# Attention in half chunks with heads by twos, and fewer routing operations a turn, in a fused attention and expert kernel

## The chip, the cores and the metric

The kernel runs on one core of one Trainium2 chip, in one launch. The metric is the time of the launch on the device in microseconds (us), the median of several runs. The engines are PE (matrix products), DVE (elementwise work and reductions), ACT (activation functions and copies), POOL (GpSimd), and SP, which here only issues DMAs. All data are fp32.

## The reference

One layer is computed: attention, then a feed-forward part with experts, each with a residual sum and a layer norm. The input `x` is 16 sequences of 512 tokens of 128 features; there are 16 heads of 8 features.

```python
q, k, v = silu(x @ Wq), silu(x @ Wk), x @ Wv            # split into heads
q, k = lrpe(q), lrpe(k)                                  # [t*cos(theta*pos), t*sin(theta*pos)], 8 -> 16
energy = einsum('bhnd,bhmd->bhnm', q, k) * tril(ones)    # no softmax
out = einsum('bhnm,bhmd->bhnd', energy, v) @ Wo
out = layernorm(out * sigmoid(x @ G1 @ G2)) * gamma + beta
x = layernorm(x + out)
...
# feed-forward: 8 experts, two for each token, at most 1280 tokens for each expert, and a shared part
probs = softmax(rmsnorm(x) @ router_w.T); top 2; weights normalised
routed = sum over both experts of weight * (silu(x @ rg) * (x @ ru)) @ rd
shared = silu(x @ sg) * (x @ su) @ sd
x = layernorm(x + shared + routed)
```

Since there is no softmax, attention is linear: the keys and values of all earlier tokens can be summed up in one small matrix for each head (a "state"), and only the tokens of one's own chunk need the masked product.

## The kernel before

**Stages.** Attention runs first, by turns of one chunk of 128 tokens (64 turns, four chunks for each sequence), and the routing of the tokens is woven into it. A loop behind attention ends the routing and the scatter of the tokens to their experts. Then come the eight experts, and last the sums and the final layer norm. The shared feed-forward part is cut into half steps (`shared_steps`, each 0.86 us of PE: one product with `sg` or `su`, or half of one with `sd`), which lie in a list, `feed`. They are taken from it by all stages: two in a turn, one in each step of the loop behind attention, and all that are left in the end stage.

**Order.** PE, DVE, ACT and POOL run their instructions in the order in which the program issues them (`manual_schedule`). The loop over `t` issues, in this order: `project(t + 2)` (products with the weights, `pq`, and their activations and copies on ACT, then `hat`, the keys and queries times cosine and sine, on DVE); a shared half step; three operations of routing (`sprinkle`); `turn_over(t + 1)` (transposes, `pt`, and on ACT the copies `kT`, `q2`, `qT`); a shared half step; a part of the output side of an earlier sequence (`after`, driven by `advance`); `energies(t)`; `values(t - 1)`; `remember(t + 1)`; two scatters on POOL; further parts of `after`; four operations of routing.

**PSUM.** There are two pools of four banks: `ps_e` for the energies (`pe`), and `ps_w` for everything else, which is taken in turn by `pq`, `pg`, `pt`, `pu`, `pout`, `pst` and the products of `after` and `route`. A new tile waits until the tile four before it has been read.

**Energies and values.** A chunk is cut into two halves of 64 tokens. The keys of every second head (the "late" heads) lie with their halves exchanged, so that the two halves of the 128 key rows hold different heads. `energies` makes three blocks of 64 queries for each group of heads: the first queries with the first keys, the last with the first, the last with the last. `q2` holds six blocks of the queries, with every second head put to zero by the two columns of `par`. The products are masked by `causal` into `et` on DVE. `values` multiplies them with padded copies of the values (`vpad`, and `vlow` for the first half), 24 products of 64 columns, and adds the state of all earlier chunks, 4 products of 128 columns.

**Memory.** `remember` multiplies keys and values of a chunk (8 products over 128 rows), masks the result with `bmask` on DVE, and adds it on POOL to the state so far. The last chunk of a sequence needs none.

**Routing.** `route` runs for three groups of sequences (0 to 5, 6 to 11, 12 to 15). It is a generator with some 33 operations, nearly all on DVE.

**Experts and end.** `clear_rows` puts rows of an expert's tile that hold no token to zero (DVE), and `turn_rows` transposes them (PE). `finish_lot` makes the last layer norm for four chunks or, for the last sequence, for one: statistics on DVE, `rstd_of` (a power on POOL) or, once the table of roots is on ACT, `rstd_by_root`, then `nb` on DVE and the output on ACT. `an_end` advances the first three unfinished lots; a lot that yields False lets the next one go.

Of the kernel before, what the change touches and what calls it, by code (L numbers as in the profile page):

```python
# [19 lines left out]
P = 128  # L20
# [18 lines left out]
PI_BELOW = 3.141592  # L39

# [6 lines left out]
def tile_kernel(  # L47
# [146 lines left out]
    with ExitStack() as ph:  # L194
# [21 lines left out]
        with tc.manual_schedule(engines=ORDERED):  # L216
# [51 lines left out]

            NVP = 4
            vpads = []  # L270
            for i in range(NVP):
                vp = cst.tile([P, 4, 4, 40], F32, name=f"vpad{i}")

                vl = cst.tile([P, 8, 40], F32, name=f"vlow{i}")
                vpads.append((vp, vl))
                if i < 2:
                    nc.gpsimd.memset(vp, 0.0)
                    nc.gpsimd.memset(vl, 0.0)
# [11 lines left out]
            for vp, vl in vpads[2:]:  # L290
                nought(vp.rearrange("p a b d -> p (a b d)"), 640)
                nought(vl.rearrange("p a d -> p (a d)"), 320)
# [24 lines left out]

        def sines(c):

            for s, (from_, scale, bias) in enumerate([(scratch[:, NC + c], -1.0, half_pi), (scratch[:, c], 1.0, 0.0)]):  # L320
                for to, n0, n1 in ((cst_tok[:, c, 0], 0, D), (cst_tok[:, c, 1, 1::2], D, D + HALF)):
                    nc.scalar.activation(
                        to[:, :, s, :], from_[:, n0:n1].rearrange("p (h d) -> p h d", d=8), AF.Sin,
                        scale=scale, bias=bias,
                    )

        def same(c):

            nc.vector.tensor_copy(
                cst_tok[:, c, 1, 0::2].rearrange("p h s d -> p h (s d)"),  # L330
                cst_tok[:, c, 0, 0::2].rearrange("p h s d -> p h (s d)"),
            )

        with tc.manual_schedule(engines=ORDERED):
# [7 lines left out]
            causal = cst.tile([P, 3, HALF], F32, name="causal")  # L342
            nc.gpsimd.tensor_tensor(causal[:, 0, 0:1], scratch[:, 0, 0:1], zcol, ALU.mult)
            nc.gpsimd.memset(causal, 1.0)
            bmask = cst.tile([P, 64], F32, name="bmask")
            nc.gpsimd.memset(bmask, 1.0)
            nc.gpsimd.affine_select(
                bmask, bmask, pattern=[[-16, 8], [0, 8]], compare_op=ALU.is_ge, fill=0.0, base=0, channel_multiplier=1
            )
            nc.gpsimd.affine_select(  # L350
                bmask, bmask, pattern=[[16, 8], [0, 8]], compare_op=ALU.is_ge, fill=0.0, base=15, channel_multiplier=-1
            )
            for block, at in ((0, 0), (0, HALF), (1, HALF), (2, 0)):
                rows = causal[at : at + HALF, block, :]
                nc.gpsimd.affine_select(
                    rows, rows, pattern=[[1, HALF]], compare_op=ALU.is_ge, fill=0.0, base=0, channel_multiplier=-1
                )
# [50 lines left out]
        hats, qkt, ets, states, gates, oTs = {}, {}, {}, {}, {}, {}  # L408


        def project(t):
# [11 lines left out]
            nc.scalar.activation(qk[:, D:].rearrange("p (h d) -> p h d", d=16), pq[:, 0:8, 16:32], AF.Silu)  # L423
            if c == 0:
# [4 lines left out]
            vp, vl = vpads[t % NVP]  # L429
            nc.scalar.copy(  # L430
                vp.rearrange("p a (c b) d -> p (a c) b d", b=2)[:, :, :, 0:8],
                pq[:, 8:16, 16:32].rearrange("p h (b d) -> p h b d", b=2),
            )
            for i in range(2):
                mine = slice(HALF * i, HALF * i + HALF)
                nc.scalar.copy(vl[mine, :, 8 * i : 8 * i + 8], pq[mine, 8:16, 16 + 8 * i : 24 + 8 * i])
# [10 lines left out]
        def turn_over(t):  # L447
# [9 lines left out]
            q2 = wk2.tile([P, 2, 6, HALF], F32, tag="q2", name=f"q2_{t}")  # L457
            halves = pt[:, 0].rearrange("p a (h n) -> p a h n", h=2)
            nc.scalar.activation(q2[:, :, 0:5:4, :], halves, AF.Copy, scale=par[:, 0:1])
            nc.scalar.activation(q2[:, :, 3:6:2, :], halves, AF.Copy, scale=par[:, 1:2])  # L460
            nc.scalar.copy(q2[:, :, 1:3, :], q2[:, :, 4:6, :])
# [4 lines left out]
        def remember(t):  # L466

            b, c = divmod(t, NC)
            hat = hats.pop(t)
            if c + 1 == NC:  # L470
                return
            vp = vpads[t % NVP][0]
            pst = ps_w.tile([P, 2, 64], F32, tag="w", name=f"pst_{t}")
            for s in range(2):
                for i in range(4):
                    nc.tensor.matmul(
                        pst[32 * i : 32 * i + 32, s, :], hat[:, 1, ds(s * P + 32 * i, 32)],
                        vp[:, 2 * s : 2 * s + 2, :, 0:8], start=True, stop=True,
                    )
            states[t] = new = wk3.tile([P, 2, 64], F32, tag="state", name=f"state_{t}")  # L480
            mask = bmask.unsqueeze(1).to_broadcast([P, 2, 64])
            if c == 0:
                nc.vector.tensor_tensor(new, pst, mask, ALU.mult)
            else:
                add = wk2.tile([P, 2, 64], F32, tag="add", name=f"add_{t}")
                nc.vector.tensor_tensor(add, pst, mask, ALU.mult)
                nc.gpsimd.tensor_tensor(new, states[t - 1], add, ALU.add)

        def energies(t):

            kT, q2, _ = qkt[t]
            pes = [ps_e.tile([P, 2, 3, HALF], F32, tag="e", name=f"pe_{t}_{g}") for g in range(4)]
            for s in range(2):
                for g in range(4):
                    rows = slice(32 * g, 32 * g + 32)
                    for i in range(2):
                        mine = slice(HALF * i, HALF * i + HALF)
# [612 lines left out]
```

## Time and profile before

| | |
|---|---|
| median of 3 runs | 874.49 us (873.55 to 876.25) |
| the profiled execution | 865.53 us |
| its span | 863.8 us |
| mean granted clock of PE | 0.988 of full |
| PE, DVE, ACT, POOL busy | 825.7, 554.2, 433.0, 337.2 us |
| attention turns | from about 15 us to 375 us |
| loop behind attention | to about 518 us |
| experts | to about 741 us |
| end stage | to 863.8 us |

In the rows of the profile, `L498` is line 498 of the kernel; `out<-in` are the program's names; `32*64 32x192` is a tile of 32 rows and 64 columns of the PE array that a moving matrix of 32 rows and 192 columns passes through. An fp32 product is carried out as two instructions, so the counts of matmuls are twice those of the code. In a group, the numbers after the bar are the busy time in us and the mean ns of one, then the idle time of the engine before them and who ended it. In a timeline, the numbers are start and duration in us. In a list of waits, they are us in total, how often, and the longest.

### The profile page before, as it was taken

The numbers are of one execution on the slowest core, as the hardware profiler recorded it, in microseconds if no ns is written. First come the engines' busy times: TensorE is split into PE (matmuls) and PEld (weight loads), VectorE is DVE, ScalarE is ACT, GpSimd is POOL, SyncE is SP. The second block draws the span as 40 slices with busy tenths as digits, with TensorE's granted clock in tenths as the row PEclk, the third lists the DMA queues.
The fourth block names the chain that finished last, engine by engine and source line by source line (L and its number), as shares of the span: only waits on it lengthen the run. The fifth ranks groups of instructions, "written<-read, shape, count | busy, mean of one in ns | idle before, by whom it ended". The sixth has DMA issues, their size and how long they took to land. (4 is left out here: it accounts for less than half of the span.)

```text
span 863.8 us, 24377 instructions
## 1 busy us (share of the span) xinstructions
PE 825.7 (96%) x9776; PEld 568.8 (66%) x9776; DVE 554.2 (64%) x1629; ACT 433.0 (50%) x1279; POOL 337.2 (39%) x451
## 2 busy tenths in 40 slices
PE   6899999989999998899999998999999999999896
PEld 4666668756766865756666665777667776755664
DVE  7887888889988788975533335444434442387754
ACT  6876776675677677544222222333333333243345
POOL 2132122221666665587666641343333433211110
PEclk9999999999999999999999999999999999999999
DMA  6011111110111110048000032231122200365211
GB/s 199 21 34 33 34 33 33 34 33 15 51 56 56 59 46 21 21 163 295 22 10 6 0 99 79 94 95 53 63 90 93 62 28 25 92 178 169 78 37 49
DMA packets 66387, 57.45 MB, mean 67 GB/s; under 512 B 6180, under 2 KB 55132, under 8 KB 66274
## 3 DMA queue, kind: packets, MB, share of 16 engines
q1 hardware_dynamic: 59474, 44.95, 17.1%
q0 software_dynamic: 6656, 10.69, 3.8%
q8 instruction: 77, 1.26, 0.6%
q10 hardware_dynamic: 144, 0.26, 0.1%
q14 instruction: 36, 0.29, 0.1%
HBM read 32.62 MB, written 26.48 MB: 68 GB/s over the span
## 5 line engine op out<-in xcount | busy, mean ns | idle before, releaser
L725 POOL DMA_INDIRECT xg_dram<-x,idx x128 | 132.3, 1034 | 42.7 <-issue 40.9
L936 POOL DMA_INDIRECT y_dram<-y,to x80 | 77.6, 970 | 155.3 <-ACT y L934 155.3
L138 ACT ACTIVATE sl<-pg 128x512 f32<-128x512 f32 x128 | 75.6, 594 | 121.4 <-PE pg L136 114.7
L150 DVE TENSOR_TENSOR h<-sl,pu 128x512 f32<-128x512 f32 x128 | 87.6, 684 | 74.8 <-PE pu L149 57.7
L136 PE MATMUL pg<-x1T,sg_sb 128*128 128x512 f32 x256 | 132.2, 598 | 0.0
L149 PE MATMUL pu<-x1T,su_sb 128*128 128x512 f32 x256 | 130.9, 593 | 0.0
L159 PE MATMUL pd<-sd_sb,h 128*128 128x128 f32 x1024 | 125.1, 279 | 5.9 <-DVE x1T L164 5.7
L505 DVE TENSOR_TENSOR et<-pe,causal 128x384 f32<-128x384 f32 x256 | 124.4, 547 | 9.1 <-PE pe L498 8.7
L159 PEld LDWEIGHTS pd<-sd_sb,h 128*128 128x128 f32 x1024 | 121.3, 195 | 12.1 <-DVE x1T L164 6.3
L1024 DVE TENSOR_TENSOR eh<-esl,peu 128x512 f32<-128x512 f32 (+1 forms) x96 | 57.5, 599 | 109.8 <-PE peu L1021 107.2
L112 POOL TENSOR_TENSOR rstd<-ve,neghalf 128x4 f32<-128x4 f32 x46 | 49.5, 1076 | 195.1 <-DVE ve L110 188.8
L930 PEld LDWEIGHTS ped<-rd,eh 128*128 128x128 f32 x640 | 84.0, 192 | 24.1 <-issue 22.0
L1019 PE MATMUL peg<-xgT,rg 128*128 128x512 f32 (+1 forms) x192 | 84.6, 522 | 0.0
L1021 PE MATMUL peu<-xgT,ru 128*128 128x512 f32 (+1 forms) x192 | 84.4, 521 | 0.0
L930 PE MATMUL ped<-rd,eh 128*128 128x128 f32 x640 | 84.3, 275 | 0.0
L1023 ACT ACTIVATE esl<-peg 128x512 f32<-128x512 f32 (+1 forms) x96 | 50.5, 526 | 57.5 <-PE peg L1019 54.8
L149 PEld LDWEIGHTS pu<-x1T,su_sb 128*128 128x128 f32 x256 | 45.9, 191 | 44.9 <-issue 39.9
L934 ACT ACTIVATE y<-ped,wt 128x128 f32<-128x128 f32 x80 | 29.4, 367 | 85.7 <-PE ped L930 85.7
L136 PEld LDWEIGHTS pg<-x1T,sg_sb 128*128 128x128 f32 x256 | 44.7, 192 | 37.4 <-issue 34.1
L415 PE MATMUL pq<-W,xT 128*128 128x384 f32 x128 | 59.9, 551 | 7.5 <-DVE h L150 3.2
L498 PE MATMUL pe<-q,kT 32*64 32x192 f32 x2048 | 62.6, 340 | 0.8 <-DVE et L505 0.8
L1021 PEld LDWEIGHTS peu<-xgT,ru 128*128 128x128 f32 x192 | 36.5, 190 | 32.2 <-issue 28.9
(181 smaller groups left out, 1250.8 us busy)
## 6 DMA issues: line engine op xcount, KB each, us to landing
y_dram<-vpad SPq DMA_DIRECT2D x16, 512.0 KB, 7.3
y<-y_dram SPq DMA_DIRECT2D x32, 256.0 KB, 3.3
xT<-xt SPq DMA_DIRECT2D x15, 384.0 KB, 2.9
xg<-xg_dram SPq DMA_DIRECT2D x8, 660.0 KB, 4.5
x<-x SPq DMA_DIRECT2D x16, 256.0 KB, 3.5
o<-res SPq DMA_DIRECT2D x15, 256.0 KB, 2.8
xg_dram<-x,idx POOLq DMA_INDIRECT x128, 2.3
rg<-rg SPq DMA_DIRECT2D x8, 256.0 KB, 4.7
```

Of the source, the lines that this page charges most:

```text
L136: nc.tensor.matmul(pg, sg_sb[:, ts(i, P)], seq, start=True, stop=True)
L138: nc.scalar.activation(sl, pg, AF.Silu)
L149: nc.tensor.matmul(pu, su_sb[:, ts(i, P)], seq, start=True, stop=True)
L150: nc.vector.tensor_tensor(h[i // half][:, i % half, :], h.pop(("s", i)), pu, ALU.mult)
L159: nc.tensor.matmul(pd, h[k][:, i - k * half, ts(c, P)], sd_sb[:, i, :], start=(i == 0), stop=(i == IS // P - 1))
L498: nc.tensor.matmul(pes[g][mine, s], kT[rows, s, mine], q2[rows, s, 3 * i : 3 * i + 3], start=(s == 0), stop=(s == 1),)
L505: nc.vector.tensor_tensor(et.rearrange("p s k n -> p s (k n)"), pes[g].rearrange("p s k n -> p s (k n)"), causal.rearrange("p k n -> p (k ...
L725: i = nc.gpsimd.indirect_dma_start(out=xg_dram[:, :], out_offset=bass.IndirectOffsetOnAxis(ap=idx[:, k, t : t + 1], axis=0), in_=x1[:, t, ...
L930: nc.tensor.matmul(pd, h[:, i, ts(c, P)], got[e][2][:, i, :], start=(i == 0), stop=(i == IR // P - 1))
L936: i = nc.gpsimd.indirect_dma_start(out=y_dram[:, :], out_offset=bass.IndirectOffsetOnAxis(ap=to[:, at : at + 1], axis=0), in_=y, in_offset ...
L1019: nc.tensor.matmul(pg[:, :n], rg_sb[:, ts(i, P)], xgTs[e][:, ds(o0, n)], start=True, stop=True)
L1021: nc.tensor.matmul(pu[:, :n], ru_sb[:, ts(i, P)], xgTs[e][:, ds(o0, n)], start=True, stop=True)
```

## The change

- The two halves of a chunk are treated as chunks of their own. `energies` makes for each half only the block of its own queries and keys, 128 columns for each product (two kinds of head by 64) in place of 192. `q2` has four blocks in place of six, and one copy on ACT falls away. `causal` is one triangle.
- `remember` keeps a state for the middle of each chunk (`mids`) besides the one for its end (`lasts`): two products of 64 rows in place of one of 128, two masked products on DVE and two sums on POOL, and also for the last chunk of a sequence (its middle alone).
- `values` adds a state for each half (8 products of 64 columns) and needs 16 other products in place of 24. There is one padded tile of values in place of two; ACT fills it by four copies of 64 rows.
- The late heads come in twos (two early, two late) in place of one by one; the host arranges `Wk`, `Wv`, `Wo` and `theta` to fit, and ACT writes the key activations by two instructions.
- A turn does two and three operations of routing in place of three and four.
- Four shared half steps are issued between clearing and transposing the rows of the first expert.
- A lot that waits for its root on POOL yields False until three half steps have begun, in place of one turn that counts as work.

In the new program's order, the loop behind attention and the four steps hold 168 shared half steps (156 before), the expert stage 3 (3 before) and the end stage 111 (123 before).

```diff
@@ project
-            vp, vl = vpads[t % NVP]
-            nc.scalar.copy(
-                vp.rearrange("p a (c b) d -> p (a c) b d", b=2)[:, :, :, 0:8],
-                pq[:, 8:16, 16:32].rearrange("p h (b d) -> p h b d", b=2),
-            )
-            for i in range(2):
-                mine = slice(HALF * i, HALF * i + HALF)
-                nc.scalar.copy(vl[mine, :, 8 * i : 8 * i + 8], pq[mine, 8:16, 16 + 8 * i : 24 + 8 * i])
+            vp, v = vpads[t % NVP], pq[:, 8:16, 16:32].rearrange("p k (u d) -> p k u d", u=2)
+            for half in range(2):
+                mine = slice(HALF * half, HALF * half + HALF)
+                for u in range(2):
+                    nc.scalar.copy(vp[mine, :, half ^ u, 8 * u : 8 * u + 8], v[mine, :, u, :])
@@ turn_over
-            nc.scalar.activation(q2[:, :, 0:5:4, :], halves, AF.Copy, scale=par[:, 0:1])
-            nc.scalar.activation(q2[:, :, 3:6:2, :], halves, AF.Copy, scale=par[:, 1:2])
-            nc.scalar.copy(q2[:, :, 1:3, :], q2[:, :, 4:6, :])
+            for i in range(2):
+                nc.scalar.activation(q2[:, :, :, i, :], halves, AF.Copy, scale=par[:, i : i + 1])
@@ remember
-            if c + 1 == NC:
-                return
-            vp = vpads[t % NVP][0]
-            pst = ps_w.tile([P, 2, 64], F32, tag="w", name=f"pst_{t}")
+            pst = [ps_w.tile([P, 2, 64], F32, tag="w", name=f"pst_{t}_{half}") for half in range(2)]
             for s in range(2):
                 for i in range(4):
-                    nc.tensor.matmul(
-                        pst[32 * i : 32 * i + 32, s, :], hat[:, 1, ds(s * P + 32 * i, 32)],
-                        vp[:, 2 * s : 2 * s + 2, :, 0:8], start=True, stop=True,
-                    )
+                    for half in range(2 if c + 1 < NC else 1):
+                        rows = slice(HALF * (half ^ i % 2), HALF * (half ^ i % 2) + HALF)
+                        nc.tensor.matmul(
+                            pst[half][32 * i : 32 * i + 32, s, :], hat[rows, 1, ds(s * P + 32 * i, 32)],
+                            vp[rows, 4 * s : 4 * s + 4, half, 0:16], start=True, stop=True,
+                        )
...
+            for half, kept in enumerate((mids, lasts) if c + 1 < NC else (mids,)):
+                kept[t] = new = wk3.tile([P, 2, 64], F32, tag=f"state{half}", name=f"state_{t}_{half}")
+                add = new if state is None else wk2.tile([P, 2, 64], F32, tag=f"add{half}", name=f"add_{t}_{half}")
+                nc.vector.tensor_tensor(add, pst[half], mask, ALU.mult)
+                if state is not None:
+                    nc.gpsimd.tensor_tensor(new, state, add, ALU.add)
+                state = new
@@ energies
-                    for i in range(2):
-                        mine = slice(HALF * i, HALF * i + HALF)
+                    for k in range(2):
+                        mine = slice(HALF * k, HALF * k + HALF)
+                        half = k ^ g % 2
                         nc.tensor.matmul(
-                            pes[g][mine, s], kT[rows, s, mine], q2[rows, s, 3 * i : 3 * i + 3],
+                            pes[g // 2, half][mine, s], kT[rows, s, mine], q2[rows, s, half],
                             start=(s == 0), stop=(s == 1),
                         )
@@ values
+            for half in range(2):
+                cols = slice(HALF * half, HALF * half + HALF)
+                state = mids.pop(t) if half else lasts.pop(t - 1, None)
+                for g in (0, 2, 1, 3) if state is not None else ():
+                    s, a = divmod(g, 2)
                     nc.tensor.matmul(
-                        pout[32 * a : 32 * a + 32, :], state[:, s, ts(a % 2, 32)], qT[:, s, :],
-                        start=True, stop=False,
+                        pout[32 * g : 32 * g + 32, cols], state[:, s, ts(a, 32)], qT[:, s, cols],
+                        start=(half == 0), stop=False,
                     )
...
@@ the turns
-                sprinkle(t, 3)
+                sprinkle(t, 2)
...
-                sprinkle(t, 4)
+                sprinkle(t, 3)
@@ finish_lot
             yield True
-            if not roots:
-                yield True
+            at = begun
+            while not roots and feed and begun < at + 3:
+                yield False
@@ the first expert
             for o0, n in parts:
                 clear_rows(0, o0, n)
+            for _ in range(4):
+                feed.pop(0)[2]()
             for o0, n in parts:
                 turn_rows(0, o0, n)
```

## The prediction

> **What bounds the kernel now.** I read the page's first part, then the waits of PE, then the busy table of two stretches of the attention stage, then PE's timeline of two turns, then the groups by shape.
>
> ```profile
> span 863.8 us, 24377 instructions
> ...
> PE 825.7 (96%) x9776; PEld 568.8 (66%) x9776; DVE 554.2 (64%) x1629; ACT 433.0 (50%) x1279; POOL 337.2 (39%) x451
> ```
>
> PE is busy for 96% of the span. Whether its few idle stretches have a cause that the change touches is told by its waits:
>
> ```profile
> PE pd L159 <- DVE x1T L164: 5.7, 3, 2.9
> PE po L555 <- ACT vlow L436: 4.2, 2, 2.1
> PE pq L415 <- DVE h L150: 3.2, 2, 1.9
> PE ept L906 <- DVE h L150: 2.5, 1, 2.5
> ```
>
> Three waits in the end stage (5.7 us), two at the exponentials of routing (4.2), two in the routing turns (3.2), one ahead of the first expert (2.5). Nothing waits turn by turn. The busy table of two stretches in the middle of attention says the same (columns: PE, weight loads, DVE, ACT, POOL, clock, DMA):
>
> ```profile
> 100.00:140.00 40.00, 40.00 (x850) 27.14 (x852) 34.46 (x109) 29.80 (x105) 8.25 (x10) 1.00 0.09 26
> 140.00:180.00 40.00, 40.00 (x864) 29.97 (x867) 32.48 (x100) 28.43 (x101) 10.14 (x12) 1.00 0.10 29
> ```
>
> PE is full; DVE has 14 to 19% left. So a saving on PE in a turn is a saving in time as long as DVE's turn shrinks with it. What the steps of a turn cost on PE is read from start to start, because matmuls overlap:
>
> ```profile
> 122.80 0.91 PE L498 MATMUL pe<-q,kT 32*64 32x192 f32 x32
> 123.63 0.43 PE L531 MATMUL pout<-et,vlow 128*32 128x64 f32 x16
> 123.88 0.63 PE L540 MATMUL pout<-et,vpad 128*32 128x64 f32 x32
> 124.33 0.41 PE L476 MATMUL pst<-vpad,hat 128*32 128x64 f32 x16
> 124.67 0.66 PE L602 MATMUL px<-ident,x 128*128 128x128 f32 x4
> ...
> 128.28 0.91 PE L498 MATMUL pe<-q,kT 32*64 32x192 f32 x32
> 129.11 0.43 PE L522 MATMUL pout<-qT,state 128*32 128x128 f32 x8
> 129.36 0.41 PE L531 MATMUL pout<-et,vlow 128*32 128x64 f32 x16
> 129.58 0.63 PE L540 MATMUL pout<-et,vpad 128*32 128x64 f32 x32
> 130.03 0.40 PE L607 MATMUL plg<-x1T,rw_sb 128*32 128x128 f32 x8
> ```
>
> Energies take 0.83 us. Values take 129.11 to 130.03, 0.92 us, with a state and 0.70 without. L540's 32 instructions of 64 columns on four tiles (128 rows by 32 columns) take 0.45, so a round over the four tiles takes 0.056 us and the instructions start 14 ns apart. The memory step (L476) is four such rounds, 0.22, but 0.34 pass before the next step: changing the tile shape costs about 0.12.
>
> **Part by part, on PE.** *Energies*, 64 turns: the same 32 instructions on the same eight tiles (32 rows by 64), with 128 columns instead of 192. By the 0.056 of 64 columns, 192 take about 0.16 a round; four rounds are 0.64 of the 0.83, and 0.19 does not depend on columns. New: 4 x 0.107 + 0.19 = 0.62. Saving 0.21 x 64 = 13.4 us. *Values*: with a state, before 4 state matmuls of 128 columns (worth eight of 64) and 24 of 64 columns, 16 rounds' worth; after, 8 state and 16 others of 64, 12 rounds. Saving 4 x 0.056 = 0.22 in 48 turns, 10.8. In the 16 first chunks 12 rounds become 10: 0.11 x 16 = 1.8. *Memory*: the three chunks that had 8 matmuls now have 16, each over 64 rows, so that eight tiles (64 by 32) can run at once. No row shows this shape. Bounds: eight at once, four rounds as now, 0; four at once, eight rounds, +0.22. I take 0, because the eight tiles of L498, also split by rows, overlap. But values (128 rows) and memory (64 rows) now differ in shape, and between them comes one more change of 0.12 (bounds 0 and 0.17, half more than read): 0.12 x 48 = 5.8. The last chunk of a sequence, which had none, gets 4 rounds and a change: 0.34 x 16 = 5.4. Sum on PE: -13.4 - 10.8 - 1.8 + 5.8 + 5.4 = **-14.8 us**; between -22 (shape changes free) and -4 (four tiles at once, 0.22 x 48 = +10.6).
>
> The Trainium skill's page "TensorE: Matmul & The Clock Gate", section "Wait — 56ns, not 53.3ns?", says that matmuls never start less than about 25 ns apart, however small. By it the 32 instructions of the new memory step would take 0.80 us, and the 48 steps 28 us more than I count, an estimate that would turn the change into a loss; the 14 ns of L540 contradict it for neighbouring tiles, and I follow the row.
>
> **On the other engines.** They matter only if they become later than PE.
>
> ```profile
> L505 DVE TENSOR_TENSOR et<-pe,causal 128x384 f32<-128x384 f32 x165 | 80.2, 547 | 7.1 <-PE pe L498 6.9
> L461 ACT COPY q<-q 128x256 f32<-128x256 f32 x42 | 17.0, 405 | 1.3
> L487 POOL TENSOR_TENSOR state<-state,add 128x128 f32<-128x128 f32 x20 | 9.1, 457 | 45.7 <-DVE add L486 21.3 <-DVE sq L593 16.4 <-DVE nb L582 5.5
> L594 DVE TENSOR_TENSOR sq<-sq,mv 128x4 f32<-128x4 f32 x10 | 4.2, 422 | 0.3
> L593 DVE TENSOR_TENSOR sq<-rstd 128x4 f32<-128x4 f32 x10 | 1.5, 153 | 0.0
> ```
>
> DVE: the four masked products of a turn go from 384 to 256 elements. With 278 ns for the 128 elements of L486 an element costs (547 - 278)/256 = 1.05 ns, so each saves 0.13 and a turn 0.54; one more product with `bmask` in every turn costs 0.28. Net -0.26 a turn, as much as PE's -14.8/64 = -0.23, so DVE keeps its distance. ACT: the copy of 405 ns goes; the keys come in two halves (0.27 to 2 x 0.215) and the values in four pieces (0.71 to 4 x 0.215), together +0.31; net -0.1 a turn. POOL: 96 state sums instead of 32, 64 x 0.457 = 29 us more, within the 13 to 15 of 40 us that it has idle in the scatter turns (busy 25.4 and 27.0 of 40 from 220 to 300); the sum for a chunk is made a turn before its values need it.
>
> One price of these sums falls on DVE. L594 takes 422 ns where L593, of the same four elements, takes 153: it runs just as POOL starts its sum, and waits 0.27. Such a hit can come in every turn: at most 64 x 0.457 = 29 us on DVE, 0.46 a turn, against the 0.9 that it has left of 5.4 (14 to 19%). So it is hidden in plain turns; in the turns with routing it is not. I take +1 us (0 to +6, the loss where a quarter of the 29 falls in full turns). The skill's "SBUF — State Buffer", section "Who interferes with whom", has this rule: a DVE instruction with two inputs in SBUF and a GpSimd one that reads SBUF block each other wholly. By it every sum that meets such an instruction would cost DVE its 0.457, rather than the 0.27 of the row.
>
> **Routing by five** operations a turn: 2 + 3 for 3 + 4. The same operations (about 0.36 each) are spread over seven turns rather than five, so DVE overruns a turn by 0.7 less. Of PE's 3.2 us at `pq`, plus 0.5 and 0.4 in the same turns, I expect half: **-2** (-4 to 0). The exponentials stay in the same turn, and with them the 4.2. The scatters of the second group start two turns later, so four more of them are left for the loop behind attention, which then takes eight more shared half steps: PE works through them as before, they are only taken from the end stage.
>
> **Rows cleared sooner.** Four shared half steps (0.86 each) go between clearing and transposing expert 0's rows. PE's wait of 2.5 at `ept` should be filled. But the first of them is a down step whose bank was last read by a DVE addition that is queued behind the clearing, so part of the wait stays in front of it. **-1** (-2.5 to 0).
>
> **The end stage.** 111 shared half steps remain instead of 123, with the same 64 rows of statistics and sums behind them. DVE waits 9.2 us there for POOL's roots (nine times, up to 1.2); now other work of the next lots is queued meanwhile, which should undo some of PE's 5.7 us at `pd`: -3 (-5.7 to 0). Against it: in the new order the last four-chunk lot and all four single lots finish behind the last down step, and ACT's four outputs (1.65 us) stand before the first single root: +1.9. Sum **-1** (-4 to +3).
>
> The opening loses two fills of 320 elements on ACT (0.46 each); the chain there goes through DVE's angles, so 0.
>
> **The sum.** -14.8 + 1 - 2 - 1 - 1 = -17.8 us. Against the profiled execution's own 865.5 (span 863.8 and 1.7 around it) that is 847.7. The median of the runs, 874.5, lies 9.0 above that execution; I keep the difference and predict **856.7 us**.
>
> **Rivals.** *Small tiles don't overlap.* The memory step runs four at a time: +10.6, so -7.2 and 867. For it: no row has 64 by 32. Against it: the eight tiles of L498. Chance 0.18. *The stalls go too.* The lighter DVE removes all of PE's waits in routing, at `ept` and at `pd`, and shape changes are free: -22 - 4 - 2.5 - 4 = -32.5, 842. For it: every one of these waits names DVE. Against it: two of them are tied to queue order. Chance 0.12. *PSUM becomes the bound: slower.* A turn now takes seven buffers from the ring of four at `ps_w`, and the next chunk's `pt` reuses the one of the first state product; so PE waits at `pt` until DVE has done four `et` and that product. Now the product is needed only at the next shared step. In the turn of 133.69 it ends at 137.72, and `pt` starts at 137.64; after the change the product ends 0.54 sooner and `pt` starts about 0.3 sooner, a margin of 0.16 us. If POOL's sums hold DVE back by more than that in every turn, PE pays the rest: from 0.16 + 17.8/64 = 0.44 on, the gain is gone; at 0.9 a turn the loss is 0.74 x 64 = 47, less 17.8, so +30 and 904. Against it: DVE has 0.9 left in a plain turn. Chance 0.06.
>
> **How the numbers follow.** Forecast 0.60 (846 to 863 by the bounds of its smaller terms); small tiles 0.18; stalls gone 0.12; ring 0.06; the rest, 0.04, is all terms cancelling within 0.3%, about what a measurement of this kernel can tell from no change. The range of 845 to 869 takes in the forecast and the small tiles, and leaves out the ring and most of the largest gain. Faster by over 0.3%: 0.60 + 0.18 + 0.12 = 0.90; same 0.04; slower 0.06.
>
> **What would show it.** In the changed profile: energies from start to start about 0.62, values about 0.70, memory about 0.34 with a gap of 0.1 before it; `et` near 413 ns; no row of PE waiting at `pt` for a state product; turns near 5.1 where they were 5.3 to 5.5. A memory step of over 0.5, or `pt` waits of tens of microseconds, would prove me wrong.

## The result, and the profile after

The changed kernel takes **866.1 us** (median of four runs, 865.7 to 866.7); the kernel before, with one more run beside it, 875.4 (873.6 to 876.9). The ratio is **0.9904** (95% interval 0.9886 to 0.9921): 9.3 us faster. The forecast was 17.8 us faster, 856.7. The direction was right and 866.1 lies within the range, but only half of the gain came.

Both kernels, run again unchanged, have two levels. In some sittings the kernel before takes about 867, in others about 874, and one chip gave both. The changed kernel moves with it:

| sitting | before | changed | ratio (95%) |
|---|---|---|---|
| first | 875.4 | 866.1 | 0.9904 (0.9886 to 0.9921) |
| second | 866.8 | 853.7 | 0.9844 (0.9827 to 0.9862) |
| third | 867.0 | 855.2 | 0.9866 (0.9832 to 0.9899) |
| fourth | 874.0 | 865.0 | 0.9882 (0.9860 to 0.9905) |

The first profile of the kernel before (865.5) is one of the quick level, its first runs (874.5) are of the slow level. The first profile of the changed kernel is of the slow level. So these two profiles, of nearly the same span, can't be subtracted; below, "quick" and "slow" name the level of a sitting.

The page and the waits of the changed kernel's first profile (in a list of waits: us in total, how often, the longest):

```profile
span 864.9 us, 25793 instructions
...
PE 821.7 (95%) x10288; PEld 559.5 (65%) x10288; DVE 538.2 (62%) x1695; ACT 414.5 (48%) x1342; POOL 361.6 (42%) x512
```

```profile
PE pout L538 <- issue: 6.0, 16, 0.5
PE pd L160 <- DVE x1T L165: 4.7, 3, 1.6
PE pst L479 <- ACT vpad L441: 3.1, 1, 3.1
PE po L553 <- ACT vpad L441: 3.0, 2, 1.9
```

New on top is a wait within the values step (`L538`) for "issue": PE stands still, and the profile shows nothing that it waits for. The busy table of the two stretches shown of before (PE, weight loads, DVE, ACT, POOL, clock, DMA):

```profile
100.00:140.00 40.00, 39.94 (x947) 26.69 (x948) 33.83 (x119) 26.95 (x109) 11.53 (x16) 1.00 0.09 26
140.00:180.00 40.00, 40.00 (x903) 29.07 (x903) 31.18 (x109) 26.47 (x107) 12.93 (x18) 1.00 0.10 30
```

PE is as full as before, and DVE and ACT have become lighter. So what counts is what PE's own steps take. PE's timeline of the two turns that were shown of before:

```profile
121.71 0.69 PE L505 MATMUL pe<-q,kT 32*64 32x128 f32 x32
122.34 0.43 PE L538 MATMUL pout<-et,vpad 128*32 128x64 f32 x16
122.58 0.29 PE L530 MATMUL pout<-qT,state 128*32 128x64 f32 x8
122.70 0.41 PE L538 MATMUL pout<-et,vpad 128*32 128x64 f32 x16
123.03 0.46 PE L479 MATMUL pst<-vpad,hat 64*32 64x64 f32 x32
123.49 0.66 PE L600 MATMUL px<-ident,x 128*128 128x128 f32 x4
124.12 0.91 PE L418 MATMUL pq<-W,xT 128*128 128x384 f32 x2
...
127.34 0.69 PE L505 MATMUL pe<-q,kT 32*64 32x128 f32 x32
127.96 0.32 PE L530 MATMUL pout<-qT,state 128*32 128x64 f32 x8
...
128.43 0.41 PE L538 MATMUL pout<-et,vpad 128*32 128x64 f32 x16
128.77 0.43 PE L479 MATMUL pst<-vpad,hat 64*32 64x64 f32 x16
129.13 0.43 PE L605 MATMUL plg<-x1T,rw_sb 128*32 128x128 f32 x8
129.48 0.91 PE L418 MATMUL pq<-W,xT 128*128 128x384 f32 x2
```

The energies take 122.34 - 121.71 = 0.63 us from start to start (before 0.83). But the memory step takes 0.46 (before 0.34), and the transposes `px` 0.63 (before 0.49). The whole turn, to 127.34, takes 5.63; before it took 5.48 (122.80 to 128.28). **A turn in which every product became smaller became longer.** In the next turn the new memory step (0.36, from 128.77 to 129.13) stands between the values and the logits `plg`, which had followed each other without a change of tile shape.

Such differences of starts, as medians over turns 14 to 31, give what each step takes in each of the four turns of a sequence (a turn goes from its energies to the next ones; its values are those of the chunk before, its memory step that of the chunk after):

| us, before / changed | first | second | third | fourth |
|---|---|---|---|---|
| energies | 0.84 / 0.62 | 0.84 / 0.62 | 0.84 / 0.62 | 0.84 / 0.62 |
| values, to the next step | 0.91 / 0.81 | 0.69 / 0.70 | 0.91 / 0.81 | 0.91 / 0.81 |
| memory, to the next step | 0.34 / 0.38 | 0.34 / 0.46 | none / 0.36 | 0.34 / 0.38 |
| `px`; `plg` | | 0.49 / 0.63 | 0.33 / 0.36 | |
| `pq`, first part and second | 0.97 / 0.97 | 0.87 / 0.97 | 0.97 / 0.97 | 0.97 / 0.97 |
| turn | 6.28 / 5.95 | 5.48 / 5.62 | 5.41 / 5.47 | 5.31 / 5.04 |

A sequence gains 0.33 - 0.14 - 0.06 + 0.27 = 0.40 us, 6.4 in 16 sequences if all were like these (the turns of the first three sequences and some turns with routing or scatters differ). The forecast for PE was 14.8.

### The profile page after: what moved, and what is told of

Read it like the earlier page. It is cut to its first block, busy times and chain, and to the rows that moved or that the text cites. A ratio compares the mean times of both kernels' runs of the same rounds, so it can differ in the third digit from the quotient of the medians.

```text
span 864.9 us, 25793 instructions
## 1 busy us (share of the span) xinstructions
PE 821.7 (95%) x10288; PEld 559.5 (65%) x10288; DVE 538.2 (62%) x1695; ACT 414.5 (48%) x1342; POOL 361.6 (42%) x512
## 5 line engine op out<-in xcount | busy, mean ns | idle before, releaser
L723 POOL DMA_INDIRECT xg_dram<-x,idx x128 | 128.9, 1007 | 38.7 <-issue 34.1
L160 PE MATMUL pd<-sd_sb,h 128*128 128x128 f32 x1024 | 122.8, 276 | 4.7 <-DVE x1T L165 4.7
L160 PEld LDWEIGHTS pd<-sd_sb,h 128*128 128x128 f32 x1024 | 119.1, 192 | 11.5 <-issue 5.7
L490 POOL TENSOR_TENSOR state<-state,add 128x128 f32<-128x128 f32 x96 | 44.1, 459 | 137.4 <-DVE add L488 131.0
L513 DVE TENSOR_TENSOR et<-pe,causal 128x256 f32<-128x256 f32 x256 | 90.5, 416 | 14.5 <-PE pe L505 13.0
L445 DVE TENSOR_TENSOR hat<-qk,cst_tok 128x512 f32<-128x512 f32 x64 | 44.9, 702 | 26.2 <-ACT qk L427 26.1
```

Of the source, the lines that this page charges most:

```text
L160: nc.tensor.matmul(pd, h[k][:, i - k * half, ts(c, P)], sd_sb[:, i, :], start=(i == 0), stop=(i == IS // P - 1))
L513: nc.vector.tensor_tensor(et.rearrange("p s i n -> p (s i) n"), pes[a, half].rearrange("p s i n -> p (s i) n"), causal.unsqueeze(1).to_bro ...
L723: i = nc.gpsimd.indirect_dma_start(out=xg_dram[:, :], out_offset=bass.IndirectOffsetOnAxis(ap=idx[:, k, t : t + 1], axis=0), in_=x1[:, t, ...
```

## The experiments

First, where the gain sits. The two halves of the change alone, and the kernel before once more:

```diff
 attention alone: the changed kernel, but
-                sprinkle(t, 2)          # and 3 further down
+                sprinkle(t, 3)          # and 4
-            for _ in range(4):
-                feed.pop(0)[2]()
-            while not roots and feed and begun < at + 3:
-                yield False
+            if not roots:
+                yield True
 rest alone: the kernel before with these edits the other way round
```

> The kernel before, unchanged, for a second profile and the span and clock of each run. The question is the 9.0 us between its profiled execution (865.5) and its runs (874.5). Theory 1 (the profiled execution was lucky): the runs show spans of about 873 us, and a profile near them shows pauses inside the values steps of turns 40 to 62, which the first profile lacked, so that the sum of those four turns' lengths is 23 us or more where it was 22.4. Theory 2 (the clock): runs of 874 show a granted clock lower by about 1% than the 0.988 of the profile. Theory 3 (profiled executions are always faster by 9): spans and times of all runs are near 865 where profiled and 874 where not, with equal turns.

Measured: 866.9, 0.9998 (0.9979 to 1.0016) of the kernel before beside it, clocks of 0.985 to 0.993 at all times. Its profile has the stages of the first one, within 0.8 us. All three theories fall as they were put: here the runs lie only 1 us above the first profile, at the same clock. What moved was the sitting.

> The changed attention with the old counts of routing operations (3 + 4 a turn), the old wait for roots and no shared half steps between clearing and transposing rows. By the forecast's own terms the three small edits bring 4 us together, so this kernel should take about 870 (4 more than the changed one's 866.1). Rival: the small edits bring nothing or cost something (their gains were read from PE waits that came back elsewhere), then 865 to 867. If the attention itself brings nothing, 874.

Measured: 862.2 where the kernel before took 867.6, 0.9934 (0.9913 to 0.9956): the attention is worth 5.4 us, in place of the 13.8 of the forecast. That agrees with the 6.4 of the table.

> The kernel before with the three small edits alone: five routing operations a turn, the roots waited for by half steps, and four shared half steps between clearing and transposing expert 0's rows. The forecast's terms give -2, -1 and -1: 4 us below the kernel before. The attention alone was 5.4 us below it (862.2 against 867.6), where the forecast had -13.8. Theory 1 (the small edits hold): ratio to the kernel before 0.995. Rival (their waits come back at other places): 0.998 to 1.002.

Measured: 859.5 where the kernel before took 866.8, 0.9930 (0.9907 to 0.9952): 7.3 us, more than the 4 of the forecast. 5.4 and 7.3 make 12.7; both together, in the same sitting as the rest alone, made 13.1.

Most of what the rest is worth lies with the clock. PE's granted clock in the profile is either full or half; half comes in stretches of 3.41 us or a multiple (but for the last one, which ends with the launch), each of which costs up to half its length, 1.7 us (an estimate, for a PE that would have been busy throughout). Between its opening and its last microseconds, the kernel before has four of them (from 78.8, 208.5, 334.8 and 812.7 us on in its second profile), the rest alone one (332.6). The distances between the four are 38, 37 and 140 times 3.413 us, so they lie on one raster. The busy tables of the stretch ahead and of the stretch itself (clock in the third column from the end), first of the kernel before (first profile), then of the rest alone at the turn of the first pair:

```profile
75.40:78.80 3.40, 1.93 (x46) 1.19 (x34) 2.89 (x7) 3.07 (x10) 1.84 (x3) 1.00 0.02 5
78.80:82.20 3.40, 3.40 (x10) 1.96 (x9) 0.69 (x1) 1.90 (x8) 0.00 (x0) 0.51 0.00 0
...
205.10:208.50 3.40, 1.50 (x58) 1.10 (x47) 3.33 (x11) 0.27 (x1) 0.00 (x0) 1.00 0.00 0
208.50:211.90 3.40, 3.40 (x16) 3.28 (x15) 3.40 (x15) 1.06 (x6) 0.00 (x0) 0.51 0.27 77
809.20:812.60 3.40, 0.93 (x9) 0.74 (x7) 3.15 (x8) 2.13 (x5) 0.00 (x0) 1.00 0.05 15
812.60:816.00 3.40, 2.95 (x14) 2.95 (x15) 2.23 (x11) 0.00 (x0) 1.01 (x1) 0.52 0.21 62
```

```profile
76.40:79.80 3.40, 1.93 (x20) 1.12 (x9) 2.42 (x6) 3.00 (x9) 1.36 (x2) 1.00 0.02 5
79.80:83.20 3.40, 3.40 (x52) 1.84 (x54) 1.60 (x4) 3.07 (x12) 0.00 (x0) 1.00 0.00 0
```

In the kernel before, the stretches ahead of those at half clock have PE busy for 57, 44 and 27%. The one near 208 goes with the routing: all five profiles with seven routing operations a turn have half clock from between 205.9 and 208.6 us on, none of the thirteen with five has. But turn 13 (around 78), which the small edits don't touch, took 9.30 us in the kernel before and 7.60 in the rest alone, with the same 57% ahead: there the stretch happened not to come. So, by the estimate, up to 5.1 of the 5.9 us between the two profiles (7.3 between the medians) are three stretches, and at least one of them went by no edit; that it went by how the wait lies on the raster is an inference. The runs of the rest alone show the price too: five of its seven have a mean granted clock of 0.994 and take 858.8 to 859.7 us, the two with 0.989 and 0.984 take 863.0 and 864.4. The Trainium skill's page "TensorE: Matmul & The Clock Gate", section "Part 1: The HAM clock gate (the "warmup" mystery)", has half clock after an idle window of about 3.4 us. Here the stretch ahead was not an idle one: PE was busy for 57% of it.

The three small edits, each undone in the changed kernel, with it as the yardstick:

> The changed kernel, unchanged, as the yardstick of the three kernels run beside it, and a third profile. In one of its two profiles PE paused within the values steps of turns 40 to 56 (96.8 us for these 16 turns), in the other not (89.4). If the pauses belong to the chip or its moment, this profile shows 89 to 90 us again where the kernel before takes 867, and about 97 where that takes 875.

> The changed kernel with seven routing operations a turn (3 + 4) instead of five; all else is kept. By the forecast five a turn bring 2 us (0 to 4). In the kernel before with the small edits the turns 34 to 39 took 36.3 us together and 59 to 61 19.0, where they took 38.1 and 20.0 with seven, so by the rows 2.7 us, of which 1.7 is a stretch of half clock. Theory 1 (worth 2 to 3 with this attention too): ratio 0.988 to 0.990. Rival (with the lighter DVE work of the changed attention nothing waits for routing; the attention alone, with seven, had 37.2 and 19.8): 1 us or less, 0.985 to 0.987.

> The changed kernel without the four shared half steps between clearing and transposing the rows of expert 0; all else is kept. By the forecast they bring 1 us (0 to 2.5). Read from the profile, they bring the wait of 2.5 us in front of expert 0 back, and with it a stretch of 3.4 us in which PE has half its clock (1.7 us more), if that stretch of low work falls so: 856 to 858 where the changed kernel takes 854. Rival (the wait only moved to the first of the four steps): 854.

> The changed kernel with the old wait for the roots of the last stage: one call of the chain instead of three shared half steps. By the forecast the new wait brings 1 us (a loss of 3 to a gain of 4). The small edits together brought 7.3 us, more than the 2.7 that the routing turns and the 1 that the rows explain, so by what is left the new wait is worth 2 to 3.5 us: 856 to 857.5 where the changed kernel takes 854. Rival (what was left is the clock: the kernel before had four stretches of half clock behind its opening, the three edits alone one): 854, with the same stretches, and an end stage as long.

The yardstick took 855.2 (0.9866) and its turns 40 to 55 89.4 us, the quick level. With seven routing operations the kernel takes 855.8, 0.9866 (0.9837 to 0.9894), in another sitting, on the chip where the changed kernel had 0.9844 in the second: worth 0 to 2, and no finer, because its profile has five stretches of half clock between the opening and the end where the yardstick's has two. Without the rows' four half steps it takes **853.2**, 0.9840 (0.9809 to 0.9871): the edit that should bring 1 us costs some. Its stages tell why: expert 0's rows are transposed 3.3 us earlier, while the stage behind the last expert becomes only 1.7 longer (111.1 for 109.4): taking four half steps (3.4 us) from the end stage shortens it by half of their length. Net, the edit costs 1.6. With the old wait for roots it takes 858.3, 0.9889 (0.9860 to 0.9918), and the end stage 111.7 for 109.4: the new wait is worth 2.3 us there; the rest of the 3.1 is spread over the span. The intervals of these ratios overlap with the yardstick's, so it is the stages that carry these two readings.

Next, why the attention gained so little. In the second turns, PE's weight loads wait; the changed kernel's waits in turn 17, and their releasers:

```profile
PEld pq L418 <- DVE add L488: 0.2, 1, 0.2
PEld px L600 <- ACT oT L544: 0.2, 1, 0.2
```

`px` and `pq` need buffers of the PSUM ring that ACT's copy of the values' result (`oT`, read from `pout`) and DVE's first product of the memory step (read from `pst`) have not yet read. Two kernels move steps to test it:

```diff
 memory first: the changed kernel, but
+                if 0 <= t + 1 < NT:
+                    remember(t + 1)        # from behind the values to here
                 if here:
                     energies(t)
 po later: the changed kernel, but
         def after(b):
+            yield                          # one empty half turn further down goes
...
+                advance(turns, "narrow")   # plg: from behind the memory step to here
                 if 0 <= t + 1 < NT:
                     remember(t + 1)
```

> The changed kernel with the memory step of the next chunk in front of the energies instead of behind the values: as many changes of tile shape, but its two PSUM buffers are read by DVE ahead of the four masked products, so that they are free earlier. Theory (in the second turn of a sequence the transposes of normed rows wait for ACT's copy of the values, which stands behind two normalizations, and the projection waits for DVE's first product of the memory step): transposes 0.49 us from start to start instead of 0.63, projection 0.87 instead of 0.97, memory 0.38 instead of 0.46: 0.32 a sequence, 5 us below the changed kernel beside it. Rival (waits only move: the masked products end 0.48 later, and the energies' banks are freed later): no gain, or a loss of up to 5 us.

> The changed kernel with two steps placed differently. The output projection of a sequence (po) is issued half a turn later, behind the memory step, so that its PSUM buffer is not held across the values and memory steps of the second turn; one empty half turn later in the same chain goes, and the gates get a third buffer. And the routing logits (plg, tiles of 128 rows by 32, as in the values) are issued ahead of the memory step instead of behind it. Theory: the ring of PSUM buffers is three deep while po is held, and that is what the transposes and the projection wait for: second turns get 0.32 us shorter (5.62 to 5.30), and third turns 0.13 (5.47 to 5.34), for one change of tile shape less: 16 x 0.45 = 7 us below the changed kernel beside it, 846 to 848 where that takes 854. Rival (the waits move to the next buffer, or DVE's chain, half a turn later, becomes late): within 2 us of the changed kernel, or slower.

Memory first: second turns became as expected (`px` 0.49, `pq` 0.87, 5.29 for 5.62), so the buffers are what they wait for. But the memory step now waits for ACT elsewhere (`PE pst <- ACT qT`, 8.0 us in 15 waits), first turns take 6.57 and third ones 6.39, and the kernel 856.6, 0.9882 (0.9861 to 0.9904): 3 us slower than the changed one. The rival held. Po later: the third turns became as expected (5.34 for 5.47; values 0.69 for 0.81, because `plg` has the tile shape of the values and needs no change), but second turns went to 8.04 with first ones at 5.24, together a loss of 1.7 us a sequence, and the kernel to 874.8, 1.0089 (1.0062 to 1.0115). That `po` held the ring is thereby not shown; its chain, half a turn later, brings waits of its own. (It fits the program's order: the reader of `po` is issued behind `px`, so `px` cannot inherit that buffer and takes the next, that of `pout`, and `pq` that of `pst`, as the releasers say.) With both memory sums in one buffer, so that a turn takes one less, no kernel was timed.

What is right in both, and the rows, make a further kernel:

```diff
 best: the changed kernel with plg ahead of the memory step, no half steps between the rows, and
             for half, a in ((0, 0), (0, 1), (1, 0)):
                 masked(half, a)
+            return lambda: masked(1, 1)    # the fourth product, called behind remember(t + 1)
```

> The changed kernel with three edits, put together from what the runs before showed: the routing logits ahead of the memory step (third turns 5.47 to 5.34, as in the kernel with po later: 16 x 0.13 = 2.1 us); the last of a turn's four masked products on DVE behind the two memory products, so that the projection of a second turn does not wait for the first of them (px to pq 0.63 to 0.49 and pq 0.97 to 0.87: 0.24 a sequence, 3.8 us); and the rows of expert 0 cleared and transposed without shared half steps between, as in the kernel before (1.7 us by the stage times of the run without them). Sum -7.6: ratio to the kernel before 0.976 to 0.978, where the changed kernel had 0.984 and 0.987. Rival (the masked product that is put back makes the last bank of the energies, or PE's values, late): the second turns gain nothing, and the ratio stays at 0.98 to 0.985.

Measured: **847.0** where the kernel before took 866.2, **0.9771** (0.9749 to 0.9793): below both kernels, as expected. But the turns bring less than was counted on. Second turns take 5.45 for 5.62 (not 5.38), for the first part of `pq` takes 0.71, where 0.65 was the aim and 0.75 the changed kernel's; and first turns take 6.03 for 5.95, for the step of `po` became longer. With the third turns' 0.14 that is 0.23 a sequence, 3.6 us in 16, where 5.9 were expected; with 1.6 for the rows it makes 5.2 of the some 7 by which the ratios differ, and the rest is not accounted for. Its second and third turn in the timeline:

```profile
124.32 0.46 PE L479 MATMUL pst<-vpad,hat 64*32 64x64 f32 x32
124.78 0.65 PE L604 MATMUL px<-ident,x 128*128 128x128 f32 x4
125.27 0.88 PE L418 MATMUL pq<-W,xT 128*128 128x384 f32 x2
...
129.55 0.41 PE L542 MATMUL pout<-et,vpad 128*32 128x64 f32 x16
129.77 0.40 PE L609 MATMUL plg<-x1T,rw_sb 128*32 128x128 f32 x8
130.10 0.43 PE L479 MATMUL pst<-vpad,hat 64*32 64x64 f32 x16
```

`px` to `pq` is 0.49, so the wait for DVE's product is gone from the list; the memory step ahead of `px` still takes 0.46, for that wait is ACT's. `plg` follows the values without a change of shape.

Last, the slow level. The changed kernel and the kernel before, unchanged:

> The changed kernel, unchanged, for a second profile beside the kernel before on the same chip. In its first profile the values steps of turns 40 to 55 paused (medians 1.42, 0.81, 1.08 and 1.59 us for the four chunks, where turns 14 to 31 take 0.81, 0.70, 0.81 and 0.81). Theory C (the pauses belong to the run or the chip: the attention alone had nearly none): the values steps are within 0.1 of the plain turns, and the kernel is 5 to 9 us below the kernel before, 858 to 862 where that takes 867. Theory D (the pauses belong to the changed kernel, by where its scatters fall after the routing by five): the values steps pause again, and the kernel takes 866 or more.

> The changed kernel, unchanged, once more, as yet another draw of the chip. Its first profile had pauses inside the values steps of turns 40 to 56 (96.8 us for 16 turns), and there the kernel before took 875; the next two profiles had none (89.4), and there the kernel before took 867. If the pauses go with the chip or its moment, the times of these 16 turns and of the kernel before stand together again: 89 to 90 with 867, or about 97 with 875. If they come and go from run to run, a profile of 97 can stand beside a kernel before of 867.

> The kernel before, unchanged, for a profile beside it. Theory (the 875 of its first runs were pauses like those of the changed kernel, which neither of its profiles showed, both of about 865.5): where its runs take about 875, its turns 40 to 56 take some 98 us instead of 90.0. Rival (before has no such pauses, and the 875 has another cause): 90.0 for these turns whatever the total.

After again was quick (853.7), after the fourth time slow (865.0, beside 874.0), and before the third time too (875.6). So theory C (by the values steps; it had the time too long, at 858 to 862) and the first theory of before the third time hold, though its pauses are smaller than expected (2.0 us in turns 40 to 55, not 8). One turn of the changed kernel, first slow (its first profile), then quick:

```profile
232.26 0.32 PE L530 MATMUL pout<-qT,state 128*32 128x64 f32 x8
232.40 0.69 PE L538 MATMUL pout<-et,vpad 128*32 128x64 f32 x8
233.50 0.33 PE L538 MATMUL pout<-et,vpad 128*32 128x64 f32 x6 [0.42 <-issue]
...
234.14 0.45 PE L479 MATMUL pst<-vpad,hat 64*32 64x64 f32 x32
```

```profile
232.12 0.32 PE L530 MATMUL pout<-qT,state 128*32 128x64 f32 x8
232.26 0.41 PE L538 MATMUL pout<-et,vpad 128*32 128x64 f32 x16
232.48 0.29 PE L530 MATMUL pout<-qT,state 128*32 128x64 f32 x8
232.60 0.46 PE L538 MATMUL pout<-et,vpad 128*32 128x64 f32 x16
232.98 0.46 PE L479 MATMUL pst<-vpad,hat 64*32 64x64 f32 x32
```

The same 48 matmuls take 0.86 us in the one and 1.88 in the other. Turns 14 to 31 of the changed kernel, without scatters, take 99.1 to 99.4 at both levels (of the kernel before, 100.8 at both); turns 40 to 55, with them, differ:

| us | before, quick | before, slow | changed, quick | changed, slow |
|---|---|---|---|---|
| turns 40 to 55 | 90.0 | 92.0 | 89.4 | 96.8 and 96.0 |
| last two turns and loop behind attention, to expert 0's transposes | 153.0 | 156.2 | 162.9 | 167.3 and 166.3 |
| experts | 219.1 | 221.0 | 219.1 | 219.1 |

```diff
 no scatter in turns: the changed kernel, but
-                    scatter_behind(oTs[(t - 1) // NC][:, ds((t - 1) % NC * P, 1)])
-                    scatter_behind()
                 # in the loop behind attention, one in every step
+                scatter_behind(latest[0] if t % 2 == 0 else None)
```

> The changed kernel with no scatter in the attention turns: all 128 are left for the loop behind attention, one an iteration instead of one in two. The total is expected later, by up to 30 us, because the last rows arrive later; it is turns 40 to 55 that are read. Theory A (the pauses of PE inside the values steps go with the scatters): the values steps take 0.81 us there as in turns 14 to 31 (medians 1.42, 0.81, 1.08 and 1.59 in the changed kernel), and four turns take 22.1 us, not 24.1. Theory B (the pauses come from the length of the dense row of short matmuls, whatever POOL does): the values steps stay near 1.1 to 1.6 and four turns near 24.

> The changed kernel with all scatters left for the loop behind attention, as another draw of the chip: its first run told nothing of the pauses, because the chip that it had showed none. Where the kernel before takes 874: theory A (the pauses go with the scatters) 89 to 90 us for turns 40 to 56; theory B (they come of the dense row of short matmuls and the chip, whatever POOL does) about 96. Where the kernel before takes 867, 89 again, which tells nothing.

> The changed kernel with the logits ahead of the memory step, the last masked product put back and the rows' four half steps undone, once more, as another draw of the chip. Where the kernel before takes 867, about 847 again (ratio 0.977). Where it takes 874, its values steps pause in turns 40 to 56 as the changed kernel's do (about 94 to 95 us for these 16 turns instead of 87.6), and it takes 857 to 859: ratio 0.981 to 0.983.

The first of them ran in a quick sitting and told nothing of the pauses (910.0, turns 40 to 55 88.5). The second ran in a slow one (933.0, where the kernel before took 874.4): its turns 40 to 55 take **88.5**, and no wait for "issue" is left in them. The waits went where the scatters went. Of this kernel, the list of waits over the whole span; of the changed one and the kernel before, slow, over 226 to 380 us:

```profile
PE pd L160 <- issue: 33.5, 40, 1.8
```

```profile
PE pout L538 <- issue: 5.3, 14, 0.5
```

```profile
PE pout L531 <- issue: 1.7, 6, 0.4
```

So theory A is shown: at the slow level PE's instruction stream pauses where POOL scatters rows. Best again, in the same slow sitting and with its scatters in the turns, took 858.0, 0.9808 (0.9777 to 0.9840): the same pauses (93.4 for 87.6), and still the fastest.

## Why the prediction had the direction right and the size wrong

**Right in the mechanism and mostly in size:** the energies (0.62 forecast, 0.62 measured), the values with a state (0.81 with the new change of shape, 0.92 - 0.22 + 0.12 = 0.82 forecast), and the eight tiles of 64 rows at once (0.38 to the next step, 0.34 forecast; four at a time would have been 0.56; half of the instructions, on four of the tiles, take 0.36 in the third turns). `et` took 416 ns (413 forecast); what POOL's sums cost DVE, the +1 of the sum, no run prices by itself. The rival of small tiles is refuted. By the Trainium skill's page "TensorE: Matmul & The Clock Gate", section "Wait — 56ns, not 53.3ns?", with about 25 ns from one matmul's start to the next, the memory step would take 0.80, an estimate. In the turn shown all its 32 instructions start within 0.24. The rival that the stalls go too did not hold: 4.7 us at `pd` and 3.0 at `po` are left. And PE's waits at `pt` for a state product stay at 0.3 us in all (0.5 in the quick profiles), so the ring rival's loss of 47 us did not come there. None of the prediction's signs of being wrong came, a memory step of over 0.5 or long waits at `pt`; it had not put down a sign for `px` and `pq`. Turns near 5.1 came only as the fourth of a sequence (5.04).

**Wrong, by its own steps:**
- *"Memory: ... one more change of 0.12 ... x 48", and "the last chunk ... 4 rounds and a change".* In the turn with the last chunk's memory step, the third, two changes come. The values were followed by `plg`, of their own shape, and the new memory step stands between. 0.12 x 16 = 1.9 us more. The runs with `plg` first show it: 0.13 to 0.14 a turn.
- *The ring, "needed only at the next shared step".* The prediction followed the ring to `pt` only. In second turns the waits stand at `px` and `pq`, for ACT's copy and DVE's product: 0.08 + 0.14 + 0.10 = 0.32 a sequence, 5.1 us in 16. (The 0.08, for ACT, goes by the releasers alone; of the 0.24 for DVE the best kernel won back 0.17.) This was the mechanism of the slower rival at another place, and it is the largest of the terms that the sum left out.
- The memory steps of the other turns, and the second's beside its wait, take 0.04 more than forecast, 1.9 in 48. With 0.7 that the energies brought more, these terms make 8.2 of the 8.4 us between -14.8 and -6.4; smaller differences, in `po` and `plg`, cancel. *The sum PE -14.8* was mis-sized; by the turns it is -6.4, and attention alone, with all it does to the other engines, measured -5.4.
- *Routing -2, rows -1, end -1.* The rows' term had the wrong sign (+1.6 by the stages), the roots were worth 2.3 in the end stage, the routing 0 to 2. Alone they brought 7.3, mostly because stretches of half clock went, which no term of the sum held; that so much came is in part luck.
- *"I keep the difference"* of 9.0 between the profiled execution and the median. It was no constant: it was the slow level, which costs the kernel before 7 to 9 us and the changed one 10 to 12. In quick sittings the change brought 11.8 and 13.1, in slow ones 9.3 and 9.0. Of the 8.5 us that the forecast lacks, about 5 are terms (8.4 too much for the attention, 3.3 too little for the small edits) and about 3 the level.

**Still open:** why a sitting is slow, and through what the scatters hold PE. POOL's scatters take as long at both levels (1004 to 1007 ns each in the changed kernel), and the profile names nothing that PE waits for. In the changed kernel's first profile the 17 waits for "issue" between 230 and 380 us end 0.6 to 1.6 us after a scatter began. A late fetch of instructions is not what shows: with the scatters behind attention, 18 of the waits, from 416 to 442 us, lie between two packets of the queue that brings one for about 250 instructions of PE (413 and 465 us), and PE runs 250 in that time. Why the changed kernel suffers more is argued only: its values and memory steps issue more short matmuls without a pause (80 in 1.19 us against 72 in 1.25 in a first turn).

## What to carry to other kernels

Count changes of tile shape over the whole new order, with both neighbours of every moved step: a step that disappears between two steps of different other shapes saves one, a step put between two of the same shape costs two. When a step takes one more buffer of a ring, go through every tile that follows it for a whole period, above all the rare ones, and ask which engine reads the buffer that each inherits. And before adding a saving to the median of the runs, take the profile and the runs from the same sitting, or the difference between them is carried over as if it were a constant.

## What the hardware showed that was not expected

- A wait of PE can cost more than its length: behind stretches in which PE was busy for 27, 44 and 57%, stretches of 3.41 us at half clock came, each worth up to 1.7 us. Another stretch at 57% was not followed by one; what decides there stays open.
- A scatter issued by POOL can hold PE's stream of matmuls, in some sittings and not in others: waits of 0.2 to 0.5 us in the values steps, of up to 1.8 in the loop behind attention, where all scatters together brought 33.5 us of them and a launch 23 us longer (933.0 for 910.0).
- Eight tiles of 64 rows by 32 columns run side by side as the eight of 32 by 64 do: 32 instructions of 64 columns and a change of shape within 0.38 us, where 16 on four of the tiles take 0.36.
